# A selective-scan stage on one core: part of the kept state's additions moved from ScalarE to GpSimd, and a few waits and tail products put into other slots

## The chip, the cores and the metric

The kernel runs on one core of a Trainium2 chip. A core has five engines that run their own instruction streams and meet through semaphores: TensorE (PE; its weight loads are listed as PEld), VectorE (DVE), ScalarE (ACT), GpSimd (POOL), and SyncE (SP), which here only issues DMAs. The metric is the device time of one execution in microseconds, as a median over several runs. The traces come from one profiled execution.

## The reference

The program is two layers on an image of 64 x 64 positions and 256 channels: a convolution with channel attention, and then, on the 4096 positions as a sequence, a bidirectional Mamba block with a small MLP, and a mixture of experts. The change touches the Mamba block alone. Cut to that block:

```python
xc, z = split(x @ in_proj_w.T)                 # 2 x 512 channels
xc = silu(conv4(xc) + conv_b)                  # 4 taps along the sequence
dt, Bm, Cm = split(xc @ x_proj_w.T)            # 16, 16, 16
dt = softplus(dt @ dt_proj_w.T + dt_proj_b)
dA  = exp(dt[..., None] * A)                   # 512 channels x 16 states
dBx = dt[..., None] * Bm[:, None, :] * xc[..., None]
h = dA_t * h + dBx_t                           # along the sequence
y = sum_over_states(h * C_t) + xc * Dp
out = (y * silu(z)) @ out_proj_w.T
# run forward and on the reversed sequence (other weights), added: m
m + mlp(layer_norm(m))                         # then x + that, and a layer norm
```

## The kernel before

**Iterations.** The sequence is cut into 8 pieces of 512 positions. `mamba_phase` runs 16 iterations i: even i are the forward direction, odd i the backward one, two for each piece. In an iteration there are 4 tiles of 128 channels (e), 4 groups of states (k), and 2 halves (j = 0, 2). This gives 32 **slots** to an iteration, numbered 0 to 31 (`at` in the code), and 512 slots in all. In each slot VectorE does one scan over 128 x 1024 elements. The 1024 are two rows of 512 behind one another: the first element of the second row has its decay forced to zero (`odd`), and the state that this row has to start from is added to its first input element instead.

**The work of one slot n**, by function:

- `inflow(n + 2)`: GpSimd makes the scan's input `dbx` from `dtxr` and `b` (L1713). `dbx` has three buffers.
- `keep(n - 1)`: ScalarE copies the last element of the previous scan's two rows to `state` (L1752).
- `decay(n + 1)`: ScalarE makes the next scan's factors `da` by two Exp activations into PSUM (L1703). `da` has two buffers.
- `bring(n + 1)`: the kept state's addition. ScalarE adds `brought`, one number to a partition, to one element of `dbx` (L1744, 128 x 1). It needs `inflow(n + 1)` done.
- `recur(n)`: VectorE's scan (L1724) and its product with `c` (L1729). In the five `POOLED` slots (4, 10, 12, 18, 28) the product is left to GpSimd in the slot after (`pooled`, L1734), and the scan writes `h` at once.
- `sum_states`: TensorE adds up the states, every second slot (L1761, with `skip` L1759 where k = 0). `h` has four buffers.
- `close`: in slots 0, 8, 16 and 24 VectorE multiplies the finished sum `y` with `z` (L1769).

**`brought`** is made for each half of an iteration by `carry` in three parts: GpSimd multiplies `aneg` with `first_r` (L1437), ScalarE takes the Exp (L1439), and GpSimd multiplies with the kept state (L1442). For the first half this stands in slots 30, 30 and 31 of the iteration before, for the second half in slots 9, 10 and 11. `first_r` comes from `load_first` (L1427), a 4 KB DMA of a 1 KB row in DRAM that SP writes before (L1414).

**`prepare`** makes the next iteration's inputs, one step to a slot: the input projection, the four taps, a Silu over `xc` in slot 8 (L1337), the projection to dt, B and C in slot 9 (L1342) and its copy (L1345) in slot 10, softplus in slots 11 to 23 with an Ln in slot 23 (L1382), and in slots 24 to 29 six pieces on GpSimd (`dt_piece`) with the DMAs that write them, the z projection's second half, and the copies of `z` (L1398). The first of the next one's steps stand in slots 27 to 31. In slot 0 ScalarE takes the Silu of both `z` tiles (L1837).

**`tail`** is the MLP with two layer norms, for one finished piece, as a generator of 39 steps. After every step it names what the next one needs ("PE", "ACT", "POOL", "DVE" or "DMA"). Lines 1853 to 1857 take one step of the oldest tail in a slot if the slot is not in that need's set in `FULL`; in the last iteration they take one in every slot. A tail is put in the queue in slot 3 of an even i. Its steps in order: mean by TensorE, the centring by VectorE (L116), a square by ScalarE, a sum by TensorE, an `eps` row by ScalarE (L125), a power by GpSimd (L132, "pow"), the product `hn` by GpSimd (L138), two activations on `hn` (L1493), `m` by GpSimd (L1498), four rounds of a `w1` product (L1506), activation (L1510) and VectorE's maximum (L1512), two rounds of a `w2` product (L1517) and VectorE's addition (L1522), and the second layer norm with its own mean, centring, square, sum, `eps`, pow, GpSimd product (`u2`) and VectorE's sum (L1529, `usum`). A TensorE product that works for it uses one PSUM buffer, so it waits for the engine that read the one before.

**What orders the work.** Instructions run on each engine in the order in which the Python loop emits them; nothing reorders them. Within a slot the order is: carry, inflow, keep, decay, bring, recur, loads (`load_dt` in slots 3 and 5 of every eight, `load_bc` in slots 24, 26, 28, 30), pooled, sum_states, close, `output`, the z Silu, `prepare` steps, dt pieces of slots 2 and 4, and last the tail's step.

The lines around the change:

```python
                bring(n + 1)
                if at == 8:
                    bring(n + 2)
...
                if tails and (i == 2 * NCH - 1 or at not in FULL[needs[0]]):
                    needs[0] = next(tails[0], None)
```

After the loop: the last sum and close, `drain` of what is left of the tails, `last_output` (L1640, L1644) and `last_tail`.

Of the kernel before, what the change touches and what calls it, by code (L numbers as in the profile page):

```python
# [14 lines left out]
FP = mybir.dt.float32  # L15
# [3 lines left out]
AF = mybir.ActivationFunctionType  # L19
ALU = mybir.AluOpType  # L20
# [4 lines left out]
P = 128  # L25
# [4 lines left out]
N = 512  # L30
# [1173 lines left out]
def mamba_phase(cx, early, w_in, w_x, w_out, w1, w2, x1d, ud, bcd, dtd, x2d, u2d, usum):  # L1204
# [11 lines left out]
    nc, tc = cx.nc, cx.tc  # L1216
    with ExitStack() as ctx:
        one = ctx.enter_context(tc.tile_pool(name="c_one", bufs=1))
        pr = ctx.enter_context(tc.tile_pool(name="c_pr", bufs=2))
        sp = ctx.enter_context(tc.tile_pool(name="c_sp", bufs=1))  # L1220
# [78 lines left out]
        def in_pair(q, e):  # L1299
            return [in_proj(q % 2, gots[q]["u"], e), in_proj(q % 2, gots[q]["u"], e + 1)]  # L1300
# [4 lines left out]
        def prepare(q):  # L1305

            d, got = q % 2, gots[q]

            ps = in_pair(q, 0)
            yield  # L1310
            yield
            xp = early.wide("xp")
            nc.scalar.copy(xp[:, :, 0:3], halo[d])
            for v in range(2):
                nc.scalar.copy(xp[:, v, 3:], ps[v])
            ps = in_pair(q, 2)
            yield
            yield
            for v in range(2):
                nc.scalar.copy(xp[:, 2 + v, 3:], ps[v])  # L1320
            nc.scalar.copy(halo[d], xp[:, :, N : N + 3])
            for _ in range(4):
                yield

            xc = None
            for e in range(ET + 1):
                if e > 0:
                    xc = got["xc"] = xc or pr.tile([P, ET, N], FP, name="xc", tag="xc")
                    nc.scalar.activation(xc[:, e - 1, :], ps, AF.Identity, bias=cx.col(f"convb{d}", e - 1))
                if e < ET:  # L1330
                    ps = mm_psum()
                    for k in range(4):
                        nc.tensor.matmul(  # L1333
                            ps, taps[d][:, 4 * e + k, :], xp[:, e, k : k + N], start=k == 0, stop=k == 3
                        )
                yield
            nc.scalar.activation(xc, xc, AF.Silu)  # L1337
            yield
            ps = mm_psum()
            nx = DR + 2 * DS  # L1340
            for e in range(ET):
                nc.tensor.matmul(ps[0:nx, :], wx[d][:, e, :], xc[:, e, :], start=e == 0, stop=e == ET - 1)  # L1342
            yield
            xd = few()[0:nx, :]
            nc.scalar.copy(xd, ps[0:nx, :])  # L1345

            at = 0 if d else DR
            nc.sync.dma_start(out=bcd[q], in_=xd[at : at + 2 * DS, :])
            yield


            r = slice(32 * d, 32 * d + DR)
            ex = dt = None
            for e in range(ET + 1):
                if e > 0:
                    ex = early.wide("ex")[:, :, 0:N] if e == 1 else ex
                    dt = dt or sp.tile([P, ET, N], FP, name="dt", tag="dt")
                    nc.scalar.activation(ex[:, e - 1, :], ps, AF.Abs, bias=cx.col(f"dtb{d}", e - 1))
                    nc.scalar.activation(dt[:, e - 1, :], ps, AF.Relu, bias=cx.col(f"dtb{d}", e - 1))
                if e < ET:  # L1360
                    ps = mm_psum()
                    nc.tensor.matmul(ps, wdt[r, P * e : P * e + P], xd[r, :], start=True, stop=True)
                yield

            nc.scalar.activation(ex, ex, AF.Exp, scale=-1.0)
            yield
            rds, sums = {}, {}
            for e in range(ET + 2):
                if e < ET:
                    rd = rds[e] = few()  # L1370
                    nc.scalar.activation(rd, ex[:, e, :], AF.Identity, scale=-1.0, bias=-1.0)
                    nc.scalar.add(rd, rd, 1.0)
                if e > 1:
                    nc.scalar.copy(dt[:, e - 2, :], sums.pop(e - 2))
                if 0 < e <= ET:
                    ps = sums[e - 1] = mm_psum()
                    for v, x in enumerate((rds.pop(e - 1), ex[:, e - 1, :], dt[:, e - 1, :])):
                        nc.tensor.matmul(ps, cx.ident, x, start=v == 0, stop=v == 2)
                yield


            nc.scalar.activation(ex, ex, AF.Ln, bias=1.0)  # L1382
            zs = in_pair(q, ET)
            yield
            got["dt"] = dt
            for at, (v, e) in enumerate(((0, 0), (1, 0), (0, 1), (0, 2), (0, 3), (1, 1))):
                dt_piece(q, v, e, ex)
                if at == 4 and q > 1:
                    load_first(q, 0)
                if at == 1:  # L1390
                    zs = in_pair(q, ET + 2)
                    if q + 1 < 2 * NCH:
                        load_u(q + 1)
                if at in (0, 2):
                    z = sp.tile([P, 2, N], FP, name="z", tag="z", bufs=3)
                    got.setdefault("z", []).append(z)
                    for f in range(2):
                        nc.scalar.copy(z[:, f, :], zs[f])  # L1398
                yield

        def dt_piece(q, v, e, ex=None, eng=nc.gpsimd):


            dt, xc = gots[q]["dt"], gots[q]["xc"]
            if v == 0:
                eng.tensor_tensor(dt[:, e, :], dt[:, e, :], ex[:, e, :], ALU.add)
                if q < 2:
                    return
                if e == 0:
                    firsts[q] = ip.tile([P, ET], FP, name="first", tag="first", bufs=1)  # L1410
                nc.gpsimd.tensor_tensor(firsts[q][:, e : e + 1], dt[:, e, 0:1], odd[:, 0:1], ALU.add)
                if e % 2:
                    first_rows[q, e // 2] = cx.rows.tile([P, 2], FP, name="first_row", tag="first_row", bufs=2)
                    nc.sync.dma_start(out=first_rows[q, e // 2], in_=firsts[q][:, e - 1 : e + 1])  # L1414
            else:
                x = few()
                eng.tensor_tensor(x, dt[:, e, :], xc[:, e, :], ALU.mult)

                eng.tensor_tensor(dt[:, e, 0:1], dt[:, e, 0:1], odd[:, 1:2], ALU.add)
                for w, piece in enumerate((dt[:, e, :], x)):  # L1420
                    nc.sync.dma_start(out=dtd[2 * q + w][e].rearrange("p j n -> (p j) n"), in_=piece)

        def load_first(q, h):

            t_ = got_first[q, h] = ip.tile([P, 4, 2], FP, name="first_r", tag="first_r", bufs=1)
            rows = first_rows.pop((q, h)).rearrange("(c j) e -> c (j e)", j=4)
            nc.sync.dma_start(out=t_.rearrange("p j e -> p (j e)"), in_=rows[:, None].to_broadcast([32, 4, 8]))  # L1427
# [263 lines left out]
        SPS = ET * SQ * 2  # L1691
        firsts, first_rows, got_first, brought = {}, {}, {}, {}
        gots, bcs, dts, m_of, das, us, ys, hs = {}, {}, {}, {}, {}, {}, {}, {}
# [13 lines left out]
        def inflow(n):  # L1707

            if n >= len(slots):
                return  # L1710
            i, e, k, j = slots[n]
            u = us[n] = up.tile([P, 2, N], FP, name="dbx", tag="dbx")
            nc.gpsimd.tensor_tensor(  # L1713
                u, dts[i, e, j][1], bcs[i, k][0][:, None, :].to_broadcast([P, 2, N]), ALU.mult
            )

        def recur(n):

# [14 lines left out]
            i, e, k, j = slots[n]  # L1733
            nc.gpsimd.tensor_tensor(hs[n], hs[n], bcs[i, k][1][:, None, :].to_broadcast([P, 2, N]), ALU.mult)  # L1734

        def bring(n):

            if n >= len(slots) or n in there:
                return
            there.add(n)  # L1740
            i, e, k, j = slots[n]
            if i < 2:
                return
            nc.scalar.activation(  # L1744
                us[n][:, 1, 0:1], us[n][:, 1, 0:1], AF.Identity, bias=brought[i, e // 2][:, e % 2, j // 2, k : k + 1]
            )

        def keep(n):

# [17 lines left out]
        def close(i, e):  # L1767
# [9 lines left out]
        AHEAD = 5  # L1777

        LATE = {0: 0, 1: 0, 2: 0, 3: 0, 4: 0, 6: 2, 7: 6, 13: 2, 14: 2, 15: 2, 16: 2}

        FULL = {
            "PE": {0, 1, 2, 3, 4, 5, 6, 7, 9, 18, 19, 20, 21, 23, 25, 27, 29},
            "ACT": {0, 6, 7, 8, 16, 17, 18, 19, 20, 21, 22, 23, 30, 31},
            "POOL": {0, 1, 2, 4, 24, 25, 26, 27, 28, 29, 30, 31},
            "DVE": {8, 16},
            "DMA": {},
# [2 lines left out]
        with tc.manual_schedule(engines=ORDERED):  # L1789
# [5 lines left out]
            for n, (i, e, k, j) in enumerate(slots):  # L1795
                at = n % SPS
# [7 lines left out]
                if n > 0:  # L1804
                    decay(n + 1)
                bring(n + 1)
                if at == 8:
                    bring(n + 2)
                recur(n)
                nxt = (i, e + 1) if e < ET - 1 else (i + 1, 0)  # L1810
                if nxt[0] < 2 * NCH:
# [26 lines left out]
                if i == 0:  # L1838
                    step(begin)
                step(prep, LATE.get(at, 1) if i == 0 else 1)  # L1840
                if at >= SPS - AHEAD and i + 2 < 2 * NCH:
# [347 lines left out]
```

## Time and profile before

| what | value |
|---|---|
| median of three runs | 4211.03 us (4209.73 to 4214.56) |
| the profiled execution: time | 4214.29 us |
| the profiled execution: span | 4212.5 us |
| first scan to end of last scan | 1995.3 to 3890.5 us |
| one iteration, i = 2 to 15 | 116.0 to 120.9 us |
| one iteration, i = 1 (no tail, nothing brought) | 115.0 us |
| scan L1724 | 432 and 80 times, 2.35 us |
| product L1729 | 432 times, 1.23 us |
| GpSimd product L1713 | 512 times, 2.36 us |
| Exp L1703 | 1024 times, 0.69 us |
| addition L1744 | 448 times, 0.28 us |
| table load on ScalarE | 1.28 us |

The span goes from the first instruction of the program to the end of the last; the time of the execution has 1.8 us around it. The durations are means or medians of the profiled execution. A slot of 3.6 us is a scan, a product and two short gaps of VectorE; in a `POOLED` slot it is the scan alone, 2.35 us, and in slots 0, 8, 16 and 24 a close of 0.68 us comes on top.

### The profile page before, as it was taken

What the parts mean: (1) busy time and instruction counts of PE and PEld (TensorE: products, weight loads), DVE (VectorE), ACT (ScalarE), POOL (GpSimd) and SP (SyncE); (2) the same over time, 40 slices, a digit from 0 to 9 for tenths busy, and PEclk for the clock granted to TensorE, in tenths of its full rate; (3) what the DMA queues carried; (4) which work ended last, traced back from release to release, by engine and by line L of the source; (5) the groups of instructions that cost most, each with busy time, mean ns of one, the idle gap of its engine ahead of it and who ended that gap; (6) DMA issues with size and microseconds to landing.
All of it is one profiled execution on the core that took longest, in us unless ns stands there. A gap on an engine that the chain in (4) does not pass through costs nothing. (4 is left out here: it accounts for less than half of the span.)

```text
span 4212.5 us, 43554 instructions
## 1 busy us (share of the span) xinstructions
PE 3616.6 (86%) x15116; PEld 1182.8 (28%) x15116; DVE 3493.8 (83%) x2898; ACT 2678.3 (64%) x4187; POOL 1739.0 (41%) x1132
## 2 busy tenths in 40 slices
PE   6679698999999999998788788878888888875798
PEld 2223242222222222222222222322222222221343
DVE  8996767879879878778899999999999999999211
ACT  1111315878878878776777777777777777774122
POOL 3200000000000000001888888888888888886000
PEclk9889798999999999999888899989899999977899
DMA  6412124000000000002334343443334443442121
GB/s 208 133 62 89 42 80 140 9 29 19 16 24 19 17 24 19 11 21 85 111 117 122 117 128 114 132 121 117 118 106 128 121 128 117 134 114 72 65 65 39
DMA packets 150532, 351.19 MB, mean 83 GB/s; under 512 B 35493, under 2 KB 44453, under 8 KB 150046
## 3 DMA queue, kind: packets, MB, share of 16 engines
q1 hardware_dynamic: 139214, 313.17, 24.2%
q0 software_dynamic: 11088, 35.14, 2.4%
q8 instruction: 121, 1.98, 0.2%
q14 instruction: 109, 0.89, 0.1%
HBM read 268.69 MB, written 79.56 MB: 83 GB/s over the span
## 5 line engine op out<-in xcount | busy, mean ns | idle before, releaser
L1713 POOL TENSOR_TENSOR dbx<-dtxr,b 128x1024 f32<-128x1024 f32 x512 | 1201.6, 2359 | 202.2 <-DVE da L1724 105.7
L997 ACT ACTIVATE e<-sc 128x1024 f32<-128x1024 f32 x1024 | 992.5, 1023 | 201.7 <-PE sc L990 158.9
L1724 DVE TENSOR_TENSOR_SCAN da<-da,state,dbx 128x1024 f32<-128x1024 f32 x432 | 1014.3, 2348 | 42.9 <-ACT state L1752 21.9
L916 DVE TENSOR_TENSOR s<-s,e 128x1024 f32<-128x1024 f32 x768 | 880.6, 1218 | 44.8 <-ACT e L997 44.3
L1703 ACT ACTIVATE da<-dtr,aneg 128x512 f32<-128x512 f32 x1024 | 708.1, 691 | 31.9 <-DMA dtr<-dtd 2.1
L990 PE MATMUL sc<-q,kS 32*128 32x512 f32 x4096 | 653.4, 643 | 9.9 <-ACT e L997 7.0
L132 POOL TENSOR_TENSOR ln_few<-ln_few,minus_half 128x4 f32<-128x4 f32 x29 | 29.4, 1012 | 1403.3 <-DMA ln_few<-ln_row 1403.3
L1729 DVE TENSOR_TENSOR h<-da,c 128x1024 f32<-128x1024 f32 x432 | 529.2, 1225 | 33.7 <-DVE da L1724 1.4
L923 PE MATMUL av<-e,vT 128*32 128x512 f32 x4096 | 548.4, 606 | 3.7 <-ACT o L929 3.7
L1761 PE MATMUL y<-h,sel 128*32 128x512 f32 x2048 | 380.7, 650 | 99.1 <-DVE h L1729 82.1
L451 PE MATMUL cv<-v,u 128*128 128x512 f32 x928 | 416.5, 609 | 45.4 <-DVE pad L272 26.1
L990 PEld LDWEIGHTS sc<-q,kS 32*128 32x128 f32 x4096 | 211.8, 183 | 454.1 <-issue 226.0
L1287 PE MATMUL mm<-u,win 128*128 128x512 f32 x496 | 254.5, 661 | 79.4 <-ACT z L1398 34.3
L548 DVE SCALAR_TENSOR_TENSOR acc<-pad,wdw_s,acc 128x768 f32<-128x768 f32 (+1 forms) x192 | 235.8, 1234 | 31.8 <-ACT acc L541 26.2
L451 PEld LDWEIGHTS cv<-v,u 128*128 128x128 f32 x928 | 179.1, 195 | 279.9 <-issue 228.9
L1752 ACT COPY state<-da 128x2 f32<-128x2 f32 x431 | 68.1, 158 | 260.7 <-DVE h L1729 260.0
L1333 PE MATMUL mm<-xp,taps 128*128 128x512 f32 x480 | 213.7, 597 | 3.8 <-DVE m L1482 3.7
L916 DVE TENSOR_TENSOR s<-e 128x1024 f32<-128x1024 f32 x128 | 150.9, 1220 | 63.6 <-ACT e L997 63.4
L1724 DVE TENSOR_TENSOR_SCAN h<-da,state,dbx 128x1024 f32<-128x1024 f32 x80 | 187.4, 2343 | 15.7 <-ACT da L1703 9.1
L923 PEld LDWEIGHTS av<-e,vT 128*32 128x32 f32 x4096 | 81.2, 108 | 395.6 <-issue 378.0
L1734 POOL TENSOR_TENSOR h<-h,c 128x1024 f32<-128x1024 f32 x80 | 188.5, 2356 | 2.1 <-ACT state L1752 2.1
L1761 PEld LDWEIGHTS y<-h,sel 128*32 128x32 f32 x2048 | 56.9, 112 | 392.5 <-DVE h L1729 188.1
(351 smaller groups left out, 3892.6 us busy)
## 6 DMA issues: line engine op xcount, KB each, us to landing
dtr<-dtd SPq DMA_DIRECT2D x128, 512.0 KB
dtxr<-dtd SPq DMA_DIRECT2D x128, 512.0 KB
b<-bcd SPq DMA_DIRECT2D x64, 256.0 KB
c<-bcd SPq DMA_DIRECT2D x64, 256.0 KB
dtd<-dt SPq DMA_DIRECT2D x64, 256.0 KB
dtd<-few SPq DMA_DIRECT2D x64, 256.0 KB
u<-uv SPq DMA_DIRECT2D x24, 640.0 KB
u<-ud SPq DMA_DIRECT2D x16, 512.0 KB
```

The costliest lines, as they stand in the source:

```text
L451: nc.tensor.matmul(rows4(ps), u[:, dy, P * ci : P * ci + P], v[:, dy : dy + HR, ci, :], start=dy + ci == 0, stop=dy == k - 1 and ci == CT - 1,
L548: nc.vector.scalar_tensor_tensor(o, src, w_ap, o, ALU.mult, ALU.add)
L916: nc.vector.tensor_tensor(z, x, y, ALU.add)
L923: nc.tensor.matmul(g.av[32 * h : 32 * h + 32, :], vT[:, kb, P * t + 32 * h : P * t + 32 * h + 32], es[h // 2][:, h % 2, :], start=kb == 0, ...
L990: nc.tensor.matmul(ps[h // 2][:, h % 2, :], kS[r, t, P * kb : P * kb + P], q_t[r, t, :], start=True, stop=True,)
L997: nc.scalar.activation(e, ps[i], AF.Exp)
L1287: nc.tensor.matmul(ps, win[d][:, t, P * e : P * e + P], u[:, t, ::-1] if d else u[:, t, :], start=t == 0, stop=t == CT - 1,)
L1703: nc.scalar.activation(da[:, v, :], dts[i, e, j][0][:, v, :], AF.Exp, scale=aneg[i % 2][:, a : a + 1])
L1713: nc.gpsimd.tensor_tensor(u, dts[i, e, j][1], bcs[i, k][0][:, None, :].to_broadcast([P, 2, N]), ALU.mult)
L1724: nc.vector.tensor_tensor_scan(das[n].rearrange("p v n -> p (v n)"), da.rearrange("p v n -> p (v n)"), u.rearrange("p v n -> p (v n)"), st ...
L1729: nc.vector.tensor_tensor(h, da, bcs[i, k][1][:, None, :].to_broadcast([P, 2, N]), ALU.mult)
L1761: nc.tensor.matmul(ys[i, e][32 * j : 32 * j + 32, :], cx.sel, hs[n + j // 2][:, j % 2, :], start=False, stop=k == SQ - 1,)
```

## The change

Five edits, all in `mamba_phase`:

1. `bring` can be emitted for GpSimd, as an addition of two 128 x 1 operands. For slots in `LONG` = {1, 9, 17, 24} `inflow` calls it itself, directly after the slot's `dbx`; the later call for the same slot does nothing, since `there` holds it. In the other slots ScalarE does it as before.
2. In slot 8, `bring(n + 2)`, that is slot 10's, is no longer called ahead; it comes in slot 9 with the ordinary call.
3. In the last six steps of `prepare` (slots 24 to 29), `load_first` of the first half stands ahead of the fourth piece (slot 27) and no longer behind the fifth (slot 28).
4. In the same steps, the two copies of a `z` tile are emitted one to a slot: in slots 24 and 25 for the first tile, 26 and 27 for the second. The second half of the z projection is emitted in slot 25 behind the copy of that slot.
5. In `FULL`, slot 24 is added for "PE" and slot 9 for "ACT": the tail takes no step that needs these there.

```diff
             for at, (v, e) in enumerate(((0, 0), (1, 0), (0, 1), (0, 2), (0, 3), (1, 1))):
+                if at == 3 and q > 1:
+                    load_first(q, 0)
                 dt_piece(q, v, e, ex)
-                if at == 4 and q > 1:
-                    load_first(q, 0)
+                if at in (0, 2):
+                    z = sp.tile([P, 2, N], FP, name="z", tag="z", bufs=3)
+                    got.setdefault("z", []).append(z)
+                if at < 4:
+                    nc.scalar.copy(z[:, at % 2, :], zs[at % 2])
                 if at == 1:
                     zs = in_pair(q, ET + 2)
                     if q + 1 < 2 * NCH:
                         load_u(q + 1)
-                if at in (0, 2):
-                    z = sp.tile([P, 2, N], FP, name="z", tag="z", bufs=3)
-                    got.setdefault("z", []).append(z)
-                    for f in range(2):
-                        nc.scalar.copy(z[:, f, :], zs[f])
                 yield
...
                 u, dts[i, e, j][1], bcs[i, k][0][:, None, :].to_broadcast([P, 2, N]), ALU.mult
             )
+            if n % SPS in LONG:
+                bring(n, True)
...
-        def bring(n):
+        def bring(n, pool=False):
...
-            nc.scalar.activation(
-                us[n][:, 1, 0:1], us[n][:, 1, 0:1], AF.Identity, bias=brought[i, e // 2][:, e % 2, j // 2, k : k + 1]
-            )
+            x, old = us[n][:, 1, 0:1], brought[i, e // 2][:, e % 2, j // 2, k : k + 1]
+            if pool:
+                nc.gpsimd.tensor_tensor(x, x, old, ALU.add)
+            else:
+                nc.scalar.activation(x, x, AF.Identity, bias=old)
...
+        LONG = {1, 9, 17, 24}
...
-            "PE": {0, 1, 2, 3, 4, 5, 6, 7, 9, 18, 19, 20, 21, 23, 25, 27, 29},
-            "ACT": {0, 6, 7, 8, 16, 17, 18, 19, 20, 21, 22, 23, 30, 31},
+            "PE": {0, 1, 2, 3, 4, 5, 6, 7, 9, 18, 19, 20, 21, 23, 24, 25, 27, 29},
+            "ACT": {0, 6, 7, 8, 9, 16, 17, 18, 19, 20, 21, 22, 23, 30, 31},
...
                 bring(n + 1)
-                if at == 8:
-                    bring(n + 2)
                 recur(n)
```

## The prediction

> **What bounds the kernel now.** I read the page first: 4212.5 us of span, VectorE (DVE) busy at nine tenths in all slices of the Mamba stage. Then the windows view of that stage, from the first scan to the last (1995 to 3891 us): DVE 1791.12 of 1896.00 us, ScalarE (ACT) 1435.84, GpSimd (POOL) 1620.72. So DVE sets the pace and only its 104.9 us of idle time can be won. Third, the list of DVE's waits in that window, and then the timelines around the longest ones.
>
> ```profile
> DVE da L1724 <- ACT state L1752: 21.9, 22, 2.0
> DVE da L1724 <- ACT dbx L1744: 14.0, 14, 4.2
> DVE xc L1769 <- PE y L1761: 11.2, 9, 3.2
> DVE h L1724 <- ACT da L1703: 9.1, 6, 2.7
> ```
>
> Each line is total, times, longest. Nearly all end on ACT: scans (L1724) wait for the exponentials (L1703) or the kept state's addition (L1744). Where "state L1752" is named, the L1744 before it ended 0.03 us ahead of the scan and is the true releaser. I added the idle time up by slot from the timeline (iteration i, slots 0 to 31). In i = 2 to 15, above the 0.03 to 0.1 us that every step has: slot 0 11.1 us, slot 2 16.5, slot 10 14.5, slot 24 6.2 (odd i only), slots 25 and 26 5.5 (even i only). An iteration without tail and brought state (i = 1) idles 2.6 us; i = 2 to 15 idle 87.3 together, so at most 87.3 - 14 x 2.6 = 51 us can go.
>
> **Slots 31 to 2**, i = 4 to 5, on POOL and ACT, then DVE:
>
> ```profile
> 2578.22 0.51 SPq L1427 DMA_DIRECT2D first_r<-first_row  x1
> ...
> 2585.28 0.22 POOL L1437 TENSOR_TENSOR brought<-aneg,first_r 128x16 f32<-128x16 f32 x1 [1.39 <-DMA first_r<-first_row]
> ...
> 2588.01 0.29 ACT L1744 ACTIVATE dbx<-dbx,brought 128x1 f32<-128x1 f32 x1 [0.76 <-POOL brought L1442]
> ...
> 2590.95 0.28 ACT L1744 ACTIVATE dbx<-dbx,brought 128x1 f32<-128x1 f32 x1
> 2591.25 1.28 ACT L1837 ACT_TABLE_LOAD   x1
> 2592.54 2.01 ACT L1837 ACTIVATE z<-z 128x1024 f32<-128x1024 f32 x2
> ...
> 2597.57 2.36 DVE L1724 TENSOR_TENSOR_SCAN da<-da,state,dbx 128x1024 f32<-128x1024 f32 x1 [1.43 <-ACT state L1752]
> ```
>
> The chain: a 4 KB DMA that lands late holds POOL, POOL holds ACT's first L1744, and ACT goes without a gap from there to the scan of slot 2.
>
> **Slots 8 to 10**, i = 5:
>
> ```profile
> 2621.70 0.29 ACT L1744 ACTIVATE dbx<-dbx,brought 128x1 f32<-128x1 f32 x1 [2.02 <-POOL dbx L1713]
> 2622.00 1.28 ACT L1337 ACT_TABLE_LOAD   x1
> 2623.29 1.91 ACT L1337 ACTIVATE xc<-xc 128x2048 f32<-128x2048 f32 x1
> ...
> 2628.08 2.35 DVE L1724 TENSOR_TENSOR_SCAN h<-da,state,dbx 128x1024 f32<-128x1024 f32 x1 [2.65 <-ACT da L1703]
> ```
>
> The early bring(10) waits 2.02 us for POOL with the Silu queued behind it. In every i from 1 to 14 that Silu's load starts 6.08 us before scan 10: the chain is rigid.
>
> **The Trainium skill.** "TensorE: Matmul & The Clock Gate" (Architectural detail) says that ScalarE and VectorE are strict FIFOs: the trace agrees, as just seen. "ScalarE: Activation LUTs" (What ACT_TABLE_LOAD costs) gives 1283 ns and a 1380 ns drain; the trace has 1.28 us and the ACTIVATE 0.01 us later, so I count 1.28. "DMA: Bandwidth & Descriptors" (Anatomy of one DMA) puts the fixed cost near 2 us; first_r needs 7.1 us from issue to POOL's start, and the measurement decides. The first page (What's actually happening) lets TensorE (PE) fall to half clock after some 3.4 us idle: here L1342 takes 5.90 us after 5.82 idle, 3.63 after 3.00. It agrees.
>
> **The change, part by part.**
>
> *load_first one slot earlier.* It now stands behind slot 27's load_dt on SP and waits for first_row (issued 2572.51, about 2 us by the page). Issue near 2575, landing near 2582 after the measured 7.1; POOL gets there at 2583.9 (end of L1419). POOL's DMA wait is gone with 1.8 us in hand. Behind it on SP the two loads of b and c of slot 28 go out 1 us later, for a chunk that starts three slots on. Slot 0: 11.1 to about 0.6, gain **10.5**. Where the carry came in time already (before i = 8, 12, 14), slot 2 waited 0.5 instead of 1.43. So slot 2 falls from 16.5 to 14 x 0.5 = 7, and by the next item further.
>
> *bring on POOL in slots 1, 9, 17, 24.* ACT loses 0.28 us each (0.25 net of overlap); POOL gains 0.19 to 0.22 each (L1419, 128x1, and L1437, 128x16, are the nearest rows; this addition itself is not in the trace, and it cannot cost below nothing, since POOL did not do it at all). In slot 17 nothing waits for ACT: zero, POOL's price as well, since slot 17's input is ready two slots ahead. Slot 1: 14 x 0.25 = 3.5 off slot 2, so slot 2 gains 16.5 - 3.5 = **13.0**. The bound below: the pattern may not be general, and only 3.5 comes.
>
> *bring(10) back in slot 9.* The Silu starts right behind decay(9). From scan 8 = 0: keep and decay 1.73, load and Silu to 4.95, keep(8) 5.1, load 6.4, decay 7.8, bring(10) 8.05. DVE is ready at 7.87 (two products, two scans, a close). Remaining wait 0.2 instead of 0.9 to 2.65, and in even i none, where the tail's VectorE product sits in slot 8 now: 14.5 to 1.4, gain **13.1**.
>
> *Slots 23 to 28.* bring(24) off ACT moves the Ln up 0.25; one z copy (0.57) and the two tail activations (1.62) leave slot 24 of even i. Slots 25 and 26: gain **5.4**. PE's second projection product of slot 25 waits for the split copy until some 0.1 us before scan 26, ends 1.7 later, then skip and sums until 4.5 us after scan 26; their buffer is written again 7.1 after it: nothing. In slot 27 the next projection waits 0.6 more, its copy comes two slots on: nothing.
>
> *The tail.* I unrolled the rule of L1853 by hand. Because each step needs a free slot, two numbers in the sets shift everything: a tail ended in slot 10 two iterations on, and now ends in slot 25; the next starts in slot 26. From the third tail on the order is fixed. Odd i: ACT eps slot 1, POOL pow 5, POOL hn 8, ACT hn 10, POOL m 12, PE w1 13, 15, 26, 28, PE w2 30. Even i: PE w2 in 8, PE mean in 10, DVE centre in 11, square 12, POOL 17 and 20, usum 24.
> - Odd slot 22 has no w2 product before the sums that close slot 24: gain **6.2**.
> - Even slots 8 to 12: w2 (8 records, 3.55 us) starts when DVE's x2 product ends, 5.1 after scan 8, and ends 8.65, at scan 10. Then L1342 3.5, skip and sums 2.8, the mean 1.85: 16.75. DVE wants it for the centring at 15.3. Five i (6 to 14) x 1.5: cost **7.5**.
> - Odd slot 10: behind L1345 and the carry's Exp stand two hn activations (1.62), so decay(12) and bring(12) end 6.1 to 7.1 after scan 10; DVE is ready at 5.9. Five times 0.7: cost **3.5**.
> - POOL in odd i, slots 2 to 16: 12 products of 2.36, dt pieces 2.9, three pooled 7.1, pow 1.0, hn and m 4.7. Walking the queue from scan 2, dbx for slot 16 is ready at 46.8 and scan 16 is due at 47.2: no slack. Between 0 and 2 us, taken 0.6 x 5: cost **3.0**.
> - SP carries the tail's DMAs along: ln_row to odd 1 and even 14, ln_inv to odd 5 and even 17, x1 to odd 10, x2d to even 10, u2d to even 24. Behind each stands a load_dt (slots 3 and 5 of every eight). The tightest is even slot 10, where the L1348 store waits for L1345 until 4.2 us after scan 10 and holds slot 11's load_dt 1.2 us; its data are wanted in slot 14. Nothing; if that cover failed, about 1 us in each even i.
> - VectorE's tail products and POOL's in even i (18 and 21 become 17 and 20) only change places: nothing.
> - Odd slot 25: the scan waits 0.1 for decay(25) where the close used to cover it, **0.5**.
> - The end: three steps of the last tail fall behind the loop. POOL's u2 product ends near 15.2 us after scan 29 (pow 5.8, about 7 for two DMAs, 2.4), usum 16.4; L1644 started at 15.73. Cost **0.7**, at most 3.
>
> Sum: 10.5 + 13.0 + 13.1 + 5.4 + 6.2 = 48.2; 7.5 + 3.5 + 3.0 + 0.5 + 0.7 = 15.2; net 33.0. Against the profiled run's 4214.3 (1.8 around its span) that is 4181.3; that run stood 3.3 above the median of the times, so **4178**.
>
> **Rivals.**
> 1. The DMA does not decide slots 0 and 2: first_r could land late again behind the big loads. For it: seven microseconds for 4 KB is queueing. Against: i = 8, 12, 14. Then those slots give 3.5 instead of 23.5: 4178 + 20 = 4198.
> 2. Waits move on. Each i gives ACT or PE a new last place, 1.8 us of them in 14 i is 25: 4203, hardly a difference.
> 3. Slower: POOL becomes the bound in odd i. hn in slot 8 blocks POOL's queue until ln_rstd has landed; my walk lets it land 7.3 us after pow. Each us beyond, less 0.4, delays scan 16 by one in five i; from 8.7 us on the kernel is slower by over 0.2%. At 10 us: 5 x 9.6 = 48, 4226. For it: SP waits for POOL up to 13.9 us elsewhere (L1421). Against: SP has no load between slots 5 and 8.
>
> **How the numbers follow.** The forecast has 0.5, rival 1 0.2, rival 2 0.12, rival 3 and other new stalls of its size 0.13, more than 48 us won 0.05. A measurement tells 0.2% (8.4 us). Faster: 0.5 + 0.2 + 0.05 and 0.03 of rival 2: 0.78; within: 0.09; slower: 0.13. The range goes from all gains without the tail's costs (4163) to the level of no change (4212), which leaves out rival 3.
>
> **What would show it.** Right: L1437 no longer waits for first_r; scan 0 idles 0.1 and scan 2 some 0.25; L1337 starts some 2 us after scan 8; slot 24 closes at once; new waits of L116 in even slot 11 and of scan 12 in odd i. Wrong: POOL's products late in odd slots 13 to 17 with ACT waiting at L1744, or first_r still named by POOL.

## The result, and the profile after

| | before | after |
|---|---|---|
| median, five runs each | 4211.03 us (4207.13 to 4215.27) | **4188.93 us** (4186.69 to 4191.71) |
| the profiled execution: time / span | 4214.29 / 4212.5 | 4186.69 / 4184.9 |
| first scan to end of last scan | 1895.2 | 1869.7 |
| what follows the last scan | 322.0 | 322.6 |
| VectorE's idle time in the scans | 104.8 | 81.8 |

The ratio is 0.9947 with a 95% interval of 0.9933 to 0.9962: 22 us less. The prediction said 4178, with a range of 4163 to 4212. Of the 27.6 us between the two spans, 25.5 lie in the scan stage and 2.8 ahead of the first scan, where the change does nothing.

In the new kernel's lines a number is shifted by a few: the scan is L1726, its product L1731, the kept state's addition L1751 on ACT and L1749 on POOL, `keep` L1757, the sums L1766, the close L1774, the z Silu L1841.

The same list of DVE's waits as before (total us, times, longest):

```profile
DVE ln_xc L116 <- PE tl L113: 15.4, 6, 3.3
DVE xc L1774 <- PE y L1766: 11.8, 7, 3.2
DVE da L1726 <- ACT da L1703: 7.3, 4, 2.4
DVE h L1726 <- ACT state L1757: 4.1, 7, 1.5
DVE da L1726 <- ACT state L1757: 3.9, 6, 1.9
DVE da L1726 <- ACT dbx L1751: 1.8, 6, 0.4
...
```

The scans' waits for ACT, 57.1 us in five lines before, have shrunk to some 18. Two waits for PE lead now; the first did not exist. The idle time by slot, i = 2 to 15, even and odd i added up, tells where:

| slot | before | after | moved by | predicted |
|---|---|---|---|---|
| 0 | 12.4 | 1.8 | -10.6 | -10.5 |
| 2 | 17.0 | 3.9 | -13.1 | -13.0 |
| 10 | 14.5 | 2.2 | -12.3 | -13.1 |
| 24 (odd) | 7.1 | 0.7 | -6.5 | -6.2 |
| 25 and 26 | 6.5 | 1.7 | -4.8 | -4.9 (5.4 less 0.5) |
| 11 (even) | 0.2 | 15.3 | +15.1 | +7.5 |
| 12 (odd) | 1.2 | 3.4 | +2.2 | +3.5 |
| 16 (odd) | 0.7 | 8.8 | +8.1 | +3.0 |
| 1 | 0.5 | 1.7 | +1.2 | - |

**Slots 31 to 2**, timeline of the new kernel, i = 4 to 5 (start, duration, engine, line; in brackets an idle time and its end):

```profile
2553.13 0.36 SPq L1414 DMA_DIRECT2D first_row<-first  x1
...
2554.20 0.55 SPq L1460 DMA_DIRECT2D dtxr<-dtd  x1
2559.68 0.51 SPq L1427 DMA_DIRECT2D first_r<-first_row  x1
2560.24 0.60 SPq L1450 DMA_DIRECT2D b<-bcd  x1
...
2566.56 0.22 POOL L1437 TENSOR_TENSOR brought<-aneg,first_r 128x16 f32<-128x16 f32 x1
...
2571.71 0.19 POOL L1749 TENSOR_TENSOR dbx<-dbx,brought 128x1 f32<-128x1 f32 x1
2572.75 1.28 ACT L1841 ACT_TABLE_LOAD   x1
...
2579.07 2.36 DVE L1726 TENSOR_TENSOR_SCAN da<-da,state,dbx 128x1024 f32<-128x1024 f32 x1 [0.29 <-ACT dbx L1751]
```

L1437 has no bracket any more: POOL does not wait for `first_r`. But `first_r` is not issued earlier. SP reaches `load_first` a slot earlier and then stands until the row is there, here from 2554.8 to 2559.7. The issue comes 6.3 us after the start of scan 27, where it came 6.6 us after it in the kernel before; over i = 2 to 13 the means are 6.7 and 6.9. What has changed is the order on SP. In the kernel before the two loads of b and c (256 KB each) go out ahead of it:

```profile
2574.37 0.76 SPq L1450 DMA_DIRECT2D b<-bcd  x1
2575.22 1.16 SPq L1450 DMA_DIRECT2D c<-bcd  x1
```

Now they follow it. By the semaphore records of the two traces `first_r` lands 6.4 us after its issue in the mean of i = 2 to 13 before, and 3.2 us after it now.

ACT's table load follows its two Exps; the addition for slot 1 is one of POOL's, in 0.19 us. The scan of slot 2 has 0.29 us left of 1.43.

**Slots 8 to 10**, i = 5, the same view:

```profile
2599.13 2.35 DVE L1726 TENSOR_TENSOR_SCAN da<-da,state,dbx 128x1024 f32<-128x1024 f32 x1
2599.44 1.42 ACT L1703 ACTIVATE da<-dtr,aneg 128x512 f32<-128x512 f32 x2
2600.87 1.28 ACT L1337 ACT_TABLE_LOAD   x1
...
2607.10 2.35 DVE L1726 TENSOR_TENSOR_SCAN h<-da,state,dbx 128x1024 f32<-128x1024 f32 x1 [0.18 <-ACT dbx L1751]
```

The Silu's load starts right behind `decay(9)`, 1.74 us after scan 8 (forecast 1.73), and scan 10 waits 0.18 us (forecast 0.2), where it was 2.65.

**Even slots 8 to 11**, i = 8, PE and DVE:

```profile
2956.07 3.52 PE L1517 MATMUL tl<-a1a,w2s 128*128 128x512 f32 x4 [3.80 <-DVE m L1522]
...
2959.43 1.88 PE L1517 MATMUL tl<-a1b,w2s 128*128 128x512 f32 x4
...
2961.24 3.63 PE L1342 MATMUL mm<-xc,wx 128*48 128x512 f32 x8
...
2966.86 1.98 PE L113 MATMUL tl<-m,mean_mat 128*128 128x512 f32 x4
...
2968.88 1.22 DVE L116 TENSOR_TENSOR ln_xc<-m,tl 128x1024 f32<-128x1024 f32 x1 [2.91 <-PE tl L113]
```

Two groups of four matmuls of one shape, 3.52 and 1.88 us: the first ran at half the pace. Its records begin 853 ns apart, the second's 430. The trace also has the clock that PE was granted, as a share of full speed: 0.56 in the mean of the first group, 1.00 in the second. The bracket shows PE idle for 3.80 us ahead of the first. L116 waits 2.91 us for the mean, and 2.8 to 3.3 in every even i from 6 to 14.

**Odd slots 15 and 16**, i = 7:

```profile
2861.44 2.36 DVE L1726 TENSOR_TENSOR_SCAN da<-da,state,dbx 128x1024 f32<-128x1024 f32 x1
2861.49 3.78 PE L1506 MATMUL tl<-hn,w1s 128*128 128x512 f32 x4 [1.61 <-DVE a1a L1512]
...
2865.20 1.94 PE L1766 MATMUL y<-h,sel 128*32 128x512 f32 x8
2867.23 0.69 DVE L1774 TENSOR_TENSOR xc<-y,z 128x512 f32<-128x512 f32 x1 [2.10 <-PE y L1766]
```

The w1 product of slot 15 could not start before DVE had read its PSUM buffer, and then took 3.78 us at half pace (granted clock 0.50). The sums that close slot 16 stand behind it. In i = 11 the same product took 1.98 us, and slot 16 did not wait.

### The profile page after: what moved, and what is told of

It is laid out like the page before. It is cut to its first block, busy times and chain, and to the rows that moved or that the text cites. A ratio compares the mean times of both kernels' runs of the same rounds, so it can differ in the third digit from the quotient of the medians.

```text
span 4184.9 us, 43554 instructions
## 1 busy us (share of the span) xinstructions
PE 3627.6 (87%) x15116; PEld 1182.5 (28%) x15116; DVE 3492.6 (83%) x2898; ACT 2668.0 (64%) x4131; POOL 1748.0 (42%) x1188
## 3 DMA queue, kind: packets, MB, share of 16 engines
q8 instruction: 121, 1.98, 0.2%
## 5 line engine op out<-in xcount | busy, mean ns | idle before, releaser
L1726 DVE TENSOR_TENSOR_SCAN da<-da,state,dbx 128x1024 f32<-128x1024 f32 x432 | 1013.9, 2347 | 15.2 <-ACT da L1703 7.3
L1731 DVE TENSOR_TENSOR h<-da,c 128x1024 f32<-128x1024 f32 x432 | 529.1, 1225 | 33.8 <-PE y L1766 1.2
L1766 PE MATMUL y<-h,sel 128*32 128x512 f32 x2048 | 391.6, 673 | 114.2 <-DVE h L1731 79.2
L1287 PE MATMUL mm<-u,win 128*128 128x512 f32 x496 | 269.0, 693 | 85.0 <-ACT state L1757 29.3
L548 DVE SCALAR_TENSOR_TENSOR acc<-pad,wdw_s,acc 128x768 f32<-128x768 f32 (+1 forms) x192 | 235.8, 1233 | 31.2 <-ACT acc L541 25.5
L1757 ACT COPY state<-da 128x2 f32<-128x2 f32 x431 | 68.3, 158 | 269.8 <-DVE h L1731 268.0
L1726 DVE TENSOR_TENSOR_SCAN h<-da,state,dbx 128x1024 f32<-128x1024 f32 x80 | 187.5, 2343 | 5.0 <-ACT state L1757 4.1
L1287 PEld LDWEIGHTS mm<-u,win 128*128 128x128 f32 x496 | 105.2, 222 | 249.8 <-issue 108.3
```

Source lines behind the costliest of these rows:

```text
L548: nc.vector.scalar_tensor_tensor(o, src, w_ap, o, ALU.mult, ALU.add)
L1287: nc.tensor.matmul(ps, win[d][:, t, P * e : P * e + P], u[:, t, ::-1] if d else u[:, t, :], start=t == 0, stop=t == CT - 1,)
L1726: nc.vector.tensor_tensor_scan(das[n].rearrange("p v n -> p (v n)"), da.rearrange("p v n -> p (v n)"), u.rearrange("p v n -> p (v n)"), st ...
L1731: nc.vector.tensor_tensor(h, da, bcs[i, k][1][:, None, :].to_broadcast([P, 2, N]), ALU.mult)
L1766: nc.tensor.matmul(ys[i, e][32 * j : 32 * j + 32, :], cx.sel, hs[n + j // 2][:, j % 2, :], start=False, stop=k == SQ - 1,)
```

## The experiments

The theory: edits 1 to 4 gain what was forecast, and the missing 11 us are two tail products that edit 5 puts into slots where PE runs at half pace. The rival: the tail's new order (edit 5) is itself the gain, by clearing slot 24, and the other edits only move waits. Medians depend on the chip (before: 4211 to 4225 us), so kernels are compared by their ratio to before on the same chip. After itself ran on one chip with the last three kernels below; for the others the ratio stands against one from another chip. Two traces of the same kernel differ by up to 8 us in stage length (1869.7 for after, 1878.1 for a later repetition), so for one place the idle time of its slots says more. The changed kernel once more:

> The changed kernel itself, beside the other three on their chip: ratio to the kernel before 0.9947 (0.993 to 0.996), as measured for the change.

It gave 0.9944 (0.993 to 0.9957), with 15.9 us in slot 11 and 12.3 in slot 16: both waits came again.

**The tail's sets, each way.** After with the sets of before (edit 5 undone):

```diff
-            "PE": {0, 1, 2, 3, 4, 5, 6, 7, 9, 18, 19, 20, 21, 23, 24, 25, 27, 29},
-            "ACT": {0, 6, 7, 8, 9, 16, 17, 18, 19, 20, 21, 22, 23, 30, 31},
+            "PE": {0, 1, 2, 3, 4, 5, 6, 7, 9, 18, 19, 20, 21, 23, 25, 27, 29},
+            "ACT": {0, 6, 7, 8, 16, 17, 18, 19, 20, 21, 22, 23, 30, 31},
```

> The changed kernel with the two sets in FULL as they were before: the tail runs at its old places, everything else stays changed. Theory A (the slots are separate accounts; the tail's new place costs what its new waits show): the waits of slot 11 in even i (15.1 us), slot 12 in odd i (3.4) and slot 16 in odd i (8.6) go, the close of slot 24 in odd i waits again (6.2), slot 26 in even i a little (2). About 19 us under the changed kernel: 4170. Rival B (the new place is part of the gain, because slots 9 and 24 have no room any more for the tail's ScalarE and TensorE steps): about 10 us over the changed kernel, 4199, with scan 10 or 11 waiting for ScalarE in odd i.

Measured: 4184.55 us, 0.991 (0.9893 to 0.9928), some 0.36% or 15 us better than after. The waits of slots 11, 12 and 16 are gone and the 9.2 us of slot 24 are back. A wait that neither theory had named takes part of the gain: 8.7 us in odd slot 1. Odd slot 10 waits for ACT as the rival had it, but for only 3 us more than in after. Timeline, i = 7, ahead of the scan of slot 1:

```profile
2815.89 2.36 POOL L1713 TENSOR_TENSOR dbx<-dtxr,b 128x1024 f32<-128x1024 f32 x1 [3.84 <-DMA dtxr<-dtd]
2818.33 0.19 POOL L1749 TENSOR_TENSOR dbx<-dbx,brought 128x1 f32<-128x1 f32 x1
...
2818.55 2.36 DVE L1726 TENSOR_TENSOR_SCAN da<-da,state,dbx 128x1024 f32<-128x1024 f32 x1 [1.87 <-POOL dbx L1749]
```

POOL's input for slot 1 waits for the big load of `dtxr`, and the addition and the scan wait with it. SP issues that load behind `load_first`, and in `load_first` SP stands until the row in DRAM has landed. SP's list of waits for after:

```profile
SPq L1427 <- DMA first_row<-first: 64.5, 21, 5.3
```

The same wait was 3.5 us in two times before. So edit 3 can delay the loads behind it by up to 5.3 us. What POOL waits for `dtxr` ahead of slot 1's input, added up from the traces, is 5.8 us before, 30.0 in after and 36.0 here. Why this order of the tail costs more in odd slot 1 than after's was not tried.

The same sets without the rest (before with the new `FULL`, the diff above reversed on the kernel before):

> The kernel before, with the new sets in FULL alone: the tail at its new places, nothing else changed. Theory A: slot 24 in odd i gains 6.2, slots 25 and 26 in even i gain some 4; slot 11 in even i costs 15, slot 16 in odd i 9, and slot 10 in even i waits longer by the 1.2 us of VectorE's sum that covered it (6); slots 0 and 2 stay. Together 20 us over the kernel before, 4231. Rival B: 5 to 10 us under the kernel before, 4203.

Measured: 4222.3, 0.9999 (0.9989 to 1.001): nothing. Slot 24 is cleared, slot 11 takes 15.9 us. The rival is out: edit 5 alone gains nothing measurable. The slower kernel that the main theory expected did not come either, since slots 0, 10, 24, 25 and 26 give back 17 us of the 21 that slots 2, 11, 12 and 16 take.

A third order: the sets of before with 22 added for PE.

```diff
-            "PE": {0, 1, 2, 3, 4, 5, 6, 7, 9, 18, 19, 20, 21, 23, 24, 25, 27, 29},
-            "ACT": {0, 6, 7, 8, 9, 16, 17, 18, 19, 20, 21, 22, 23, 30, 31},
+            "PE": {0, 1, 2, 3, 4, 5, 6, 7, 9, 18, 19, 20, 21, 22, 23, 25, 27, 29},
+            "ACT": {0, 6, 7, 8, 16, 17, 18, 19, 20, 21, 22, 23, 30, 31},
```

> The changed kernel, with ScalarE's set in FULL as before and TensorE's as before but slot 22 added instead of slot 24: the tail stays 64 slots long at its old places, and only the second w2 product moves from odd slot 22 to 24, the mean to 26, the centring to 27. Theory A: as with the sets of before, without the 6.2 us of slot 24 in odd i: 4164. Rival B: no better than the changed kernel, 4189 or more. A third outcome: w2 in slot 24 makes a new wait behind it (the z projection of slot 25 comes later by 3.5 us), then 4170 and a wait of DVE in odd slots 26 to 28.

Measured: 4198.86, 0.9942 (0.9927 to 0.9957). Slot 24 closes nearly at once (1.3 us) and slots 11 and 16 are clear, but the centring waits 13 us in odd slot 27, its mean being behind the z projection and a w2 product that is again at half pace after 3.80 us of idle time. Slot 1 idles 17.8 us, nearly all of it in waits for POOL. No gain over after.

**Is it the half pace?** After, with dummy matmuls that keep PE busy ahead of the two slow products (their result is not used):

```diff
+                if 4 <= i < 2 * NCH - 1 and (at == 8 and i % 2 == 0 or at == 15 and i % 2):
+                    ps = mm_psum()
+                    for v in range(WARM[at]):          # WARM = {8: 4, 15: 3}
+                        nc.tensor.matmul(ps, cx.ident, gots[i]["xc"][:, 2, :], start=True, stop=True)
```

> The changed kernel with extra TensorE products whose result nobody reads: four (8 records) in even slot 8 and three (6 records) in odd slot 15, ahead of the tail's product there, so that TensorE does not sit idle before it. Theory C (w2 in slot 8 and w1 in slot 15 run at half clock because of the idle time before them, 3.8 and 1.6 us): L1517 takes 3.6 instead of 5.4 us, the wait of L116 in even slot 11 falls from 3.0 to about 1.3 (8 us less in all), and that of the close in odd slot 16 from 2.1 to below 0.5 (7 us less): 4175. Rival D (the products are late for what stands ahead of them in TensorE's queue, not for the clock): no gain or up to 4 us slower, 4189 to 4193.

Measured: 4185.78, 0.9914 (0.9896 to 0.9931). Timeline, i = 8:

```profile
2960.40 3.70 PE L1861 MATMUL mm<-xc,ident 128*128 128x512 f32 x8
...
2964.27 1.98 PE L1517 MATMUL tl<-a1a,w2s 128*128 128x512 f32 x4 [0.17 <-DVE m L1522]
...
2966.09 1.88 PE L1517 MATMUL tl<-a1b,w2s 128*128 128x512 f32 x4
...
2973.52 1.98 PE L113 MATMUL tl<-m,mean_mat 128*128 128x512 f32 x4
2975.54 1.22 DVE L116 TENSOR_TENSOR ln_xc<-m,tl 128x1024 f32<-128x1024 f32 x1 [1.37 <-PE tl L113]
```

The w2 product now takes 3.70 us, nearly the 3.55 of the forecast, and L116 waits 1.37: slot 11 falls from 15.3 to 7.1 us, near the 7.5 that the prediction had. For slot 11 the half pace is shown to be the missing half. In slot 15 the dummies took 2.8 to 4.5 us, in two i mostly at half pace. In four of the five i the quick w1 product behind them (1.88 us) so ended later than without them, and slot 16 took 11.8; in i = 9, where the dummies took 2.8, the close waited 0.32.

For slot 16 the trace of the sets alone on the kernel before decides. There the same w1 product starts at the same place, 0.03 to 0.05 us after scan 16 in i = 5 to 13. It takes 1.98 us in two of these i and 2.6 to 2.7 in three, never 3.78, and the close of slot 16 waits 0 to 0.14 us. So the late place alone costs next to nothing; the half pace makes the wait.

**One edit undone at a time.** `load_first` back behind the fifth piece (edit 3):

```diff
-                if at == 3 and q > 1:
-                    load_first(q, 0)
                 dt_piece(q, v, e, ex)
+                if at == 4 and q > 1:
+                    load_first(q, 0)
```

> The changed kernel with load_first back behind the fifth piece (slot 28). Theory A (the late landing of first_r decides slots 0 and 2): POOL waits for first_r again in slots 30 and 31, slot 0 idles some 10 us more and slot 2 some 9 more over the iterations: 20 us over the changed kernel (ratio to the kernel before about 0.9995). Rival E (the early load only moves the wait: SP now stands at load_first until the row it reads has landed, up to 5 us, and holds the loads behind it): no more than 5 us slower than the changed kernel, ratio 0.996, and scan 1 waits less for POOL.

Measured: 4213.57, 0.9977 (0.997 to 0.9984), 0.3% or 13 us worse than after, where theory A had 20. Slot 0 idles 10.9 us again, slot 2 12.3, and POOL waits for `first_r` 11 times, 27.0 us together; it lands 6.5 us after its issue in the mean of i = 2 to 13. A third of slot 2's gain stays without this edit. POOL's wait for `dtxr` ahead of slot 1 is 6.4 us here, so its 30.0 in after come from edit 3.

Slot 10's addition ahead in slot 8 again (edit 2):

```diff
                 bring(n + 1)
+                if at == 8:
+                    bring(n + 2)
                 recur(n)
```

> The changed kernel with slot 10's bring called ahead in slot 8 again. Theory A: the Silu waits behind it until POOL's product for slot 10 is done, in odd i about 3.0 us after scan 8 instead of 1.75, so scan 10 waits 1.2 us more in six odd i, and in even i (product done at 2.0, VectorE's tail product as a cover) nothing: 7 us slower than the changed kernel. Rival F (the whole of slot 10's gain hangs on this call): 12 us slower, 0.9 and more in every i.

Measured: 4203.39, 0.9947 (0.9931 to 0.9964). In the trace slot 10 takes 13.3 us instead of 2.2, most of it in odd i. So the edit takes 11 us off that slot, where the prediction had 13.1. The ratio does not show them. 11 us are 0.26%; the ratio differs by 0 to 0.03% from the two of after, and with intervals of 0.13 to 0.17% to each side some 0.2% could hide in that. What the edit is worth in time stays open.

No addition on POOL (edit 1):

```diff
-        LONG = {1, 9, 17, 24}
+        LONG = set()
```

> The changed kernel with LONG empty: ScalarE does all the additions. Theory A: 0.25 us each on ScalarE's chain where it bounds: slot 2 in 14 i (3.5), slots 10 and 25 in odd i (1.7 each): 7 us slower. Rival G (what ScalarE saves, GpSimd loses: scan 1 then waits for nothing of GpSimd's): no difference, within 2 us.

Measured: 4222.83, 0.9994 (0.9986 to 1.0002). **The largest miss:** one 0.28 us addition in four slots is worth 0.47%, 20 us, where theory A had 7. Slot 2 alone idles 25.4 us, more than in the kernel before. Timeline, i = 6 to 7, ahead of the scan of slot 2:

```profile
2820.81 9.30 POOL L1713 TENSOR_TENSOR dbx<-dtxr,b 128x1024 f32<-128x1024 f32 x4 [3.39 <-DMA dtxr<-dtd]
2823.20 0.29 ACT L1751 ACTIVATE dbx<-dbx,brought 128x1 f32<-128x1 f32 x1 [2.21 <-POOL dbx L1713]
2823.51 1.28 ACT L1841 ACT_TABLE_LOAD   x1
...
2829.83 2.36 DVE L1726 TENSOR_TENSOR_SCAN da<-da,state,dbx 128x1024 f32<-128x1024 f32 x1 [2.69 <-ACT dbx L1751]
```

POOL waits for the late `dtxr`, ACT's addition for slot 1 waits 2.21 us for POOL, and the z Silu and all that follows stand behind that addition. What the edit removes is less ACT's 0.28 us than its standing in wait: with the addition on POOL, ACT goes on to the Silu whether POOL is ready or not. And since most of the lateness comes from edit 3 (6.4 us without it, as shown above, 35.8 here), edit 3 needs edit 1. A kernel without both was not run, so what edit 1 is worth by itself is not known.

The two copies of a z tile in one slot again (edit 4):

```diff
-                if at < 4:
-                    nc.scalar.copy(z[:, at % 2, :], zs[at % 2])
...
+                if at in (0, 2):
...
+                    for f in range(2):
+                        nc.scalar.copy(z[:, f, :], zs[f])
```

> The changed kernel with both z copies of a tile in one slot (24, 26), as before. Theory A: VectorE's sum (even i) and the close cover ScalarE's two copies in slot 24 now, so nothing returns in slots 25 and 26: within 2 us of the changed kernel. Rival H (the split copies are what emptied slots 25 and 26): 5 us slower, with scans 25 and 26 of even i waiting for ScalarE.

Measured: 4200.73, 0.9938 (0.9922 to 0.9955): no loss. Slots 25 and 26 stay as clear as in after (2.2 and 1.7 us together). With edit 5 undone and edit 4 in, they are clear too (1.6). So either edit is enough there beside the others, and edit 4 adds nothing that this can measure.

**Better than both?** After with `load_first` in slot 28, but ahead of the fifth piece, to relieve SP:

```diff
-                if at == 3 and q > 1:
+                if at == 4 and q > 1:
                     load_first(q, 0)
```

> The changed kernel with load_first in slot 28 ahead of the fifth piece: on SP behind the two loads of b and c of slot 28, still ahead of the next wait for POOL. Theory I (SP stands at load_first until the row that it reads has landed, and what stands behind it is late: the load of dtxr for the next iteration's second input, and so scan 1): first_r goes out at the same time, b and c no longer wait, the load_dt of slot 29 goes out about 1 us earlier, POOL's wait for dtxr in slot 0 shrinks by that; 1 to 3 us under the changed kernel, and scan 1 waits for GpSimd at most in i = 2 and 3. Rival J (the landing itself is what is late, SP's order is not): same as the changed kernel, within 1 us, with the same issue times of load_dt.

Measured: 4205.55, 0.9966 (0.9952 to 0.9979), 0.2% worse than after on this chip, where theory I had 1 to 3 us less. POOL's list of waits:

```profile
POOL brought L1437 <- DMA first_r<-first_row: 19.5, 8, 3.1
```

The wait is back in eight iterations. In i = 5 `first_r` is issued 1.5 us later than in after, in i = 7 only 0.35 us later, and yet POOL waits 2.07 us there. It now stands on SP behind the two 256 KB loads of b and c, not ahead of them. Over i = 2 to 13 it lands 5.9 us after its issue, in after 3.2 and in after's second trace 3.2, though it is issued only 0.4 us later than in the latter. So it is the place behind the two loads that delays it.

Then the tail spread so that no product for it stands in slot 8 and none of its VectorE steps in slots 11 and 27:

```diff
-            "PE": {0, 1, 2, 3, 4, 5, 6, 7, 9, 18, 19, 20, 21, 23, 24, 25, 27, 29},
-            "ACT": {0, 6, 7, 8, 9, 16, 17, 18, 19, 20, 21, 22, 23, 30, 31},
+            "PE": {0, 1, 2, 3, 4, 5, 6, 7, 8, 9, 18, 19, 20, 21, 23, 25, 27, 29},
+            "ACT": {0, 6, 7, 8, 16, 17, 18, 19, 20, 21, 22, 23, 30, 31},
...
-            "DVE": {8, 16},
+            "DVE": {8, 11, 16, 27},
```

> The changed kernel with other sets in FULL: TensorE's as before plus slot 8, ScalarE's as before, VectorE's plus 11 and 27. The tail is 64 slots long as in the changed kernel, but no w2 product stands ahead of L1342 in even slot 8, the centring follows its mean by two slots (12, 28), and no product stands in odd slot 15. Theory C (slot 11 waits for a half-clock w2 and the queue behind it; slot 16 for a half-clock product in slot 15): the waits of slots 11 and 16 (15.3 and 8.8 us) go, slot 16 to below 2; two activations in odd slot 9 make scan 11 wait about 1 us in six i. 17 us under the changed kernel, ratio 0.9907. Rival K (GpSimd's overload in odd i, which this keeps, is the cause of slot 16, and new places give new waits): 5 us under at most.

Measured: **4181.92 us, 0.9914** (0.99 to 0.9927), 0.3% or 14 us under after on the same chip, faster than both kernels, and level with the two runs above at 0.991. Its mean and its centring, i = 8:

```profile
2966.85 1.98 PE L113 MATMUL tl<-m,mean_mat 128*128 128x512 f32 x4
...
2970.17 1.19 DVE L116 TENSOR_TENSOR ln_xc<-m,tl 128x1024 f32<-128x1024 f32 x1
```

The w2 products have moved to slots 29 and 31, the centring comes a slot after its mean, and L116 has no bracket. The w1 product still runs at half pace (3.78 us), but starts at the beginning of odd slot 15 and not of slot 16; the close of slot 16 waits no more. So slot 16 needs both: take away either the half pace (i = 11, and the sets alone) or the late start (here), and the wait is gone. The price is 8.7 us in odd slot 11 and 5.7 in odd slot 14, scans waiting for ACT. Both together:

> Both together: the sets of spread and load_first as in first28. If they are separate accounts: 18 to 20 us under the changed kernel, ratio 0.990. If the wait only moves: as spread alone or worse.

Measured: 4189.6, 0.9933 (0.992 to 0.9947): slot 28 costs 0.2% here as well.

## Why the prediction was right, and where it was off

**The gains, 48.2 forecast (47.7 with the 0.5 of odd slot 25), 47.3 in the table: the sizes are right.** Slots 0, 2, 10, 24 and 25 with 26 each came within 0.8 us, and the signs in the trace are those named: no wait of L1437, the Silu's load at +1.74 us. (The prediction has this load 6.08 us ahead of scan 10 in every i from 1 to 14 of the kernel before; in i = 2 it is 6.71.)

**"Issue near 2575, landing near 2582 after the measured 7.1": wrong, and the gain of slots 0 and 2 came all the same.** The forecast moved the issue 3.2 us forward and kept the landing time. The issue hardly moved: from the row's own DMA to `first_r` it took 6.5 us (2553.13 to 2559.68), where the prediction had some 2.5. The landing became shorter instead, 3.2 us in the mean and not 6.4, since `first_r` now goes out ahead of the loads of b and c. The prediction named this order only as a price for those loads, and the queueing of `first_r` only in its first rival. Once L1437 no longer waits, the size of the gain follows from the trace before; that it no longer waits was luck, by the reason that the forecast gave.

**Their shares among the edits: partly wrong.** The step that priced the addition at "14 x 0.25" counted a duration and left out the wait in front of it; undone, the edit costs 20 us, because slot 2 hangs on the wait for POOL too. And slots 25 and 26 did not need the split copy.

**"Behind it on SP the two loads of b and c go out 1 us later": too low.** SP waits in `load_first` up to 5.3 us for its own row. In i = 4 the load of b goes out 4.1 us later than before, counted from scan 27, and that of `dtxr` 1.4 us. In after this costs 1.2 us (slot 1), in two other orders of the tail 9 to 18.

**Even slot 11, 7.5 forecast, 15.1 measured: right place, half the size.** The term that failed is "w2 (8 records, 3.55 us)". It took 5.24 us in i = 8, since PE had stood idle for 3.80. The prediction had quoted this very rule from the Trainium skill, "TensorE: Matmul & The Clock Gate" (What's actually happening: half rate after an idle window of some 3.4 us), and shown it on L1342; it did not apply it to the product that it moved behind an idle PE. The rest of the term was a little too long: skip and sums took 2.1 us and not 2.8 (and the terms add up to 16.8, not 16.75), and DVE was ready at 14.9 and not at 15.3. So of the 1.7 us on w2 the wait grew by 1.4 in i = 8, from 1.5 to 2.9; in the five i it is 2.8 to 3.3. With the dummies the forecast's size came out.

**Odd slot 12, 3.5 forecast, 2.2 measured:** right.

**"POOL in odd i ... cost 3.0" at slot 16: the wrong mechanism.** Slot 16 costs 8.1, but it waits for PE's sums behind the half-pace w1 product of slot 15, which the forecast counted at nothing. Scan 16 does not wait for POOL, so the third rival did not occur either.

**The end, 0.7 forecast, 0.6 measured.** The other traces have 322 to 327 us there, so this is no confirmation.

**The sum.** The terms take 33.7 us off VectorE's idle time in the scans (33.0 and the 0.7 of the end); the traces show 23.0. The two undersized terms, 7.6 and 5.1 us, are more than the difference; slot 12 and small items in other slots give the rest back.

## What to carry to other kernels

An instruction that waits at the head of an in-order queue costs what stands behind it, not its duration: moving a 0.28 us addition to the engine that it waits for was worth 20 us here, beside an edit that had made that engine late. When work for PE is moved, read the idle time ahead of its new place and take the duration that the trace shows after such a pause. Moving a small transfer ahead of large ones can shorten it even where it goes out no earlier, and can delay what stands behind it if the issuing engine has to wait for its source. So edits that look independent should be undone one at a time.

## What the runs showed of the hardware that was not expected

- PE at half pace does not need a pause directly ahead of the instruction: in odd slot 15 w1 products ran with records 853 ns apart after a gap of only 1.6 us (and after 0.4 us in i = 5). The w1 product of slot 13, with no gap ahead of it, was at half pace too. In i = 11 the product of slot 15 ran at 430 ns after the same 1.6 us. So the gap directly ahead does not tell the pace.
- A 4 KB load landed 3.2 us after its issue in the mean when it went out ahead of two 256 KB loads on the same queue, and 5.9 to 6.5 us after it when it went out behind them.
- Filling an idle PE with unused matmuls made the kernel quicker where the idle stretch was free: 3.70 us of dummies in even slot 8 took 1.5 us off the product behind them.
- The 128 x 1 addition takes 0.19 us on GpSimd and 0.28 us on ScalarE.
